# Attention in rounds of eight score tiles, and changed orders of issue in the first stage, in a four-layer float32 kernel

## The chip, the cores and the metric

The kernel runs on one core of one Trainium2 chip. Its time is the device time of one execution in microseconds (us): the median of three runs is 2684.59, from 2683.01 to 2685.78. A profile is taken of one further execution.

The engines' names are those of the profile: PE is TensorE (matmul), PEld its weight loads, DVE is VectorE, ACT is ScalarE, POOL is GpSimd, SP is the engine that issues the DMAs. SBUF is the on-chip working memory, PSUM the memory into which TensorE writes.

## What is computed

The reference passes x (4 images of 512 channels, 64 x 64 positions, float32) through four layers. Only the first matters here:

```python
t = jnp.einsum('oc,bchw->bohw', w_qkv, x)          # key, query, value: 64 channels each
scores = jnp.einsum('bdk,bdq->bkq', key_, query)   # 4096 x 4096 for each image
attn = jax.nn.softmax(scores, axis=1)
out = jnp.einsum('bdk,bkq->bdq', value, attn)
out = jnp.einsum('oc,bchw->bohw', w_out, out)
return scale * out + x
```

Layer 1 is a bottleneck of convolutions whose weights are mixed from eight experts by a router; layer 2 is a linear attention with softplus features; layer 3 is a gate by the sigmoid of a discounted cumulative sum along rows and columns, added to its input.

## The kernel before

The four images (batches) are worked on one after the other. TensorE's order is written out by hand for the whole program (`manual_schedule` of PE around everything, L1074). ACT's and DVE's orders are written out in some stretches only. Where an engine's order is not written out, a planner orders its instructions before the launch, by their place in the program and by its own estimate of when each is ready. In every case an engine carries out its instructions strictly in the order that was fixed, and a semaphore wait of one holds all behind it. Memory is handed out by the planner too: a tile of a pool with n buffers waits for an earlier tile's last reader.

**First stage, `Projections`.** An image is four pairs of blocks (`xs[0]` to `xs[3]`, 128 x 4 x 1024). The keys and queries of two pairs are made together from seven products (numbers 1 to 7) instead of eight, so some inputs are differences that DVE makes first. `steps` (L229) is the written order: a digit is a product on TensorE (L304); `t4`, `n5` and so on are two subtractions on DVE (L252), `t` for this couple of pairs, `n` for the next; `v` is a value product (L260), `cp` its two copies by ACT (L266), `tr` its turning by TensorE and two copies by DVE; `seed`, `e2`, `e3` are copies of the accumulator `y` by ACT; `c11` is four copies by ACT from the first half of the PSUM tile `zy` into the keys (L290); `c22` is one DVE addition of the other half of `zy` and e3 into the queries (L326); `c12` and `c21` are DVE's two remaining results. Product 3 writes the half of `zy` that c22 reads. Two key copies of the second couple are left for later (`key_copies`), those of the first are the step `k`. DVE's and ACT's orders are written out here.

**Attention, `layer0`.** There are 128 tiles: 4 query pairs of 32 key tiles. `scores(i)` makes a tile of 128 keys by 1024 queries: two score matmuls into a PSUM pair (pool tag "s", three buffers), an exponential on ACT (L368) into slot i % 12 of the ring, and the running sum on DVE (L373). `values(i)` multiplies the ring's slot by the values into a bank that collects a query pair (two buffers). The profile shows each matmul as two records, so a tile of scores is four records and a tile of values four. The tiles go in groups of six: the scores of group g, then the values of group g-1. When a pair's values are complete, `sums` follows (two `den` matmuls with ones, L396, a reciprocal on DVE, L399, and three small DVE operations), and for the first two pairs four `out_step`s: an out product (L424) into a PSUM pair, and its addition to x on DVE (L429). They are kept in the list `late`, and up to two are issued in each group, between the scores and the values. The first group is followed by the left key copies and, in batch 0, by the router's transposes (L172). `pool` (L442) is one ACT pass over a piece of x in each of eight groups. The sum product of the last pair, `inverse_sums`, stands before the values of tile 124. In this loop only PE's and ACT's orders are written out; DVE's is the planner's.

**Last stage, `layer3`.** Eight blocks go through products, scans and gates; `last_steps` (L1015) is the written order for the last block of an image, of which only the gate is left. Among DVE's steps there are `g first` (needs sigmoid 0 on ACT), `g second` (three operations and an output) and `g third` (needs sigmoid 1; three operations and an output). The first products of the next image stand among them.

**The ACT table.** The exponentials need a function table that the sigmoid's place doesn't hold; its load is issued at the start of `layer0` (L342). In batch 0 the load follows a square root.

Of the kernel before, what the change touches and what calls it, by code (L numbers as in the profile page):

```python
# [22 lines left out]
NT = HW // P  # L23
TPB = NB // P
NPAIR = NBLK // 2
# [9 lines left out]
BQ2, BK2 = 48, 49  # L35
NPRM = 50
RING = 12

R2 = 2 * ROWS

# [5 lines left out]
def unshifted(ctx: ExitStack, tc: tile.TileContext, fits, x, wqkv_t, wout_t, router_t,  # L46
# [3 lines left out]
    nc = tc.nc  # L50
# [9 lines left out]
    def pair_psum(name):  # L60
        return ps.tile([P, 2, NB], F32, tag="s", name=name, bufs=3)

    def bank(name, shape=(P, NB)):
        return ps.tile(list(shape), F32, tag="acc", name=name)

    def four(name):
        return fourp.tile([P, 2, NB], F32, tag="four", name=name)

    def block(name, shape=(P, NB)):
        return blkp.tile(list(shape), F32, tag="blk", name=name)  # L70
# [31 lines left out]
    def col(i, n=1):  # L102
        return prm_sb[:, i:i + n]
# [46 lines left out]
    groups = [(0, 1, G1, B1, M1, V1), (1, 1, G2, B2, M2, V2), (2, KC, G3, B3, M3, V3)]  # L150
# [15 lines left out]
    def router_of_values():  # L166


        wo_t = pair_psum("wo_t")
        wot_sb = block("wot_sb")  # L170
        for kc in range(KC):
            nc.tensor.transpose(wo_t[:, 0, kc * P:(kc + 1) * P], wout_sb[:, kc * P:(kc + 1) * P], ident)  # L172
        nc.vector.tensor_copy(wot_sb, wo_t[:, 0, :])

        def products():
            wr = pair_psum("wr_p")[:, 0, 0:E]
            for kc in range(KC):
                nc.tensor.matmul(wr, wot_sb[:, kc * P:(kc + 1) * P], router_sb[:, kc, :],
                                 start=kc == 0, stop=kc == KC - 1)
            nc.vector.tensor_scalar(wr_sb, wr, col(SCALE), 1.0 / HW, ALU.mult, ALU.mult)  # L180
        return products

    def load_experts(b, j, n, pool, tag, pack=True):
        if pool is xpool:
            ex = places[NPAIR][:, 0:n, :].rearrange("p n (q g c) -> p n q g c", q=4, g=2)
            nc.sync.dma_start(ex, packed[:, j:j + n])
        elif pack:
            ex = pool.tile([P, n, 4, 2, P], F32, tag=tag, name=f"ex_{b}_{j}")
            nc.sync.dma_start(ex, packed[:, j:j + n])
        else:  # L190
            ex = pool.tile([P, n, E, P], F32, tag=tag, name=f"ex_{b}_{j}")
            nc.sync.dma_start(ex, experts[j:j + n].rearrange("n p e c -> p n e c"))
        return b, j, n, ex
# [18 lines left out]
    class Projections:  # L212
# [14 lines left out]
            nc.vector.tensor_tensor(self.w[3], a12, self.w[6], ALU.subtract)  # L227

        def steps(self, b):  # L229
            first = "v1 cp01 5 1 seed v2 t6 t4 n5 6 n6 e2 2 7 e3 c11 c22 tr01 n7 4 c21 3 c12 n4"  # L230
            if b == 0:
                first = "zero v0 1 seed t5 v1 cp01 t6 5 2 t7 t4 6 e2 v2 7 e3 c11 c22 tr01 n5 n6 n7 4 c21 3 c12 n4"
            return first.split(), "5 1 seed k v3a 6 e2 2 v3b cp23 7 e3 c11 c22 tr23 4 c21 3 c12".split()

        def key_copies(self):
            while self.left:
# [102 lines left out]
    def layer0(b, xs, pro):  # L339


        tc.keep_in_program_order(nc.scalar.preload_act_table_set("natural_log_exp_and_others"))  # L342
        ex0 = load_experts(b, 0, KC, wlate, "late")
        key = bigp.tile([P, HW], F32, tag="big", name=f"key_{b}")
        qv = bigp.tile([P, 2, NPAIR * NB], F32, tag="big", name=f"qv_{b}")
# [3 lines left out]
        with tc.manual_schedule(engines={mybir.EngineType.DVE, mybir.EngineType.Activation}):  # L349
            pro.sum_weights()  # L350
            for pair, steps in zip(((0, 1), (2, 3)), pro.steps(b)):
                pro.products(xs, pair, steps, key, qry, vt)
        ringx = places[NPAIR].rearrange("p i (h n) -> p i h n", h=2)
        ring = [pro.sums[:, i] for i in range(4)] + [ringx[:, i] for i in range(4)] + pro.fours

# [4 lines left out]
        def scores(i):  # L360
            pr, kt = divmod(i, NT)
            s = pair_psum(f"s_{b}_{i}")
            for h in range(2):
                r = slice(h * D, (h + 1) * D)
                nc.tensor.matmul(s[:, h, :], key[r, kt * P:(kt + 1) * P],  # L365
                                 qry[r, pr * NB:(pr + 1) * NB], start=True, stop=True)
            p = ring[i % RING]
            nc.scalar.activation(p, s, AF.Exp)  # L368
            if kt == 1:
                accs[pr] = four(f"acc_{b}_{pr}")  # L370
                nc.vector.tensor_tensor(accs[pr], ring[(i - 1) % RING], p, ALU.add)
            elif kt > 1:
                nc.vector.tensor_tensor(accs[pr], accs[pr], p, ALU.add)  # L373

        def values(i):
            pr, kt = divmod(i, NT)
            if kt == 0:
                avs[pr] = bank(f"av_{b}_{pr}")
            for h in range(2):
                nc.tensor.matmul(avs[pr][h * D:(h + 1) * D, :], vt[:, kt, :], ring[i % RING][:, h, :],  # L380
                                 start=kt == 0, stop=kt == NT - 1)
            if kt < NT - 1:
                return None
            if pr < NPAIR - 1:
                av = block(f"avsb_{b}_{pr}")
                nc.scalar.copy(av, avs[pr])
                avs[pr] = av
            return pr
# [3 lines left out]
        def inverse_sums(pr):  # L392
            acc = accs[pr]
            den = bank(f"den_{b}_{pr}")
            for h in range(2):
                nc.tensor.matmul(den[h * D:(h + 1) * D, :], ones[:, 0:D], acc[:, h, :],  # L396
                                 start=True, stop=True)
            recs[pr] = block(f"rec_{b}_{pr}")
            nc.vector.reciprocal(recs[pr], den)  # L399

        def sums(pr, early=True):
            if early:
                inverse_sums(pr)
            av, rec = avs[pr], recs[pr]
            o = block(f"o_{b}_{pr}")
            if pr >= NPAIR - 2:
                i = pr - NPAIR + 2
                nc.vector.scalar_tensor_tensor(o, av, 1.0, rec, ALU.mult, ALU.mult, accum_out=osum[:, i:i + 1])
            else:
                nc.vector.tensor_tensor(o, av, rec, ALU.mult)  # L410
            outs[pr] = o
            if early:
                sum_range(pr)
# [19 lines left out]
        def out_step(pr, m):  # L433
            add_out(pr, m, out_product(pr, m))
# [5 lines left out]
        def pool(pr, kc):  # L440
            xm = xs[pr][:, kc, :]
            nc.scalar.activation(xm, xm, AF.Copy, accum_out=pool_acc[:, kc, pr:pr + 1])  # L442

        groups = [range(i, min(i + RING // 2, NPAIR * NT)) for i in range(0, NPAIR * NT, RING // 2)]
        late = []
        with tc.manual_schedule(engines={mybir.EngineType.Activation}):
            for g, group in enumerate(groups):
                for i in group:
                    scores(i)
                if 1 < g < 2 + 2 * KC:  # L450
                    pool(NPAIR - 2 + (g - 2) // KC, (g - 2) % KC)
                if g == 0:
                    pro.key_copies()
                    if b == 0:
                        router = router_of_values()
                    continue
                for _ in range(2):
                    if late and late[0][0] < g:
                        late.pop(0)[1]()
                for n, i in enumerate(groups[g - 1]):  # L460
                    if g == len(groups) - 1 and n == 4:
                        inverse_sums(NPAIR - 1)
                    pr = values(i)
                    if pr is not None:
                        late.append((g, lambda pr=pr: sums(pr)))
                        if pr < NPAIR - 2:
                            late += [(g + 1, lambda pr=pr, m=m: out_step(pr, m)) for m in range(KC)]
                if b == 0 and g == 1:
                    router()
        assert not [t for t in late if t[0] < len(groups) - 1], late  # L470


        pooled = small.tile([P, KC], F32, tag="pooled", name=f"pooled_{b}")
# [10 lines left out]

        pr = NPAIR - 1
        ex4 = load_experts(b, 4, 3, bigp, "big")
        for i in groups[-1]:
            values(i)
        ex7 = load_experts(b, 7, 3, xpool, "x")
        wcq = bigp.tile([P, NPIECE + 1 + 4 * NPAIR, P], F32, tag="big", name=f"wc_{b}")  # L490
# [376 lines left out]
    def layer3(b, xs, value_product, value_add, left, weights, wcq):  # L867
# [3 lines left out]
        weights, down, _ = weights  # L871
# [105 lines left out]
        class Gates(Block):  # L977
# [18 lines left out]
            def add_x(self, i):  # L996
# [17 lines left out]
                       ("s3", "s second"))  # L1014
        last_steps = (("g5", "l rows 1", "l rows 0"), ("g1", "g seed", "v 0"), ("g6", "g copy_out 2", "l turn 1"), ("g2",),  # L1015
                      ("g7", "g copy_out 3", "l columns 1", "g fourth", "l turn 0", "l columns 0", "l sigmoid 1",
                       "l sigmoid 0", "v 2"), ("g4",), ("g3", "x", "g third", "g first", "g second"))
        pro = None
        ys = [(pr, m) for pr in range(1, NPAIR) for m in range(KC)]
        nxt = []  # L1020
# [53 lines left out]
    with tc.manual_schedule(engines={mybir.EngineType.PE}):  # L1074
        pro = Projections(0)
        for b in range(B):
            convs = layer1(b, xs, *layer0(b, xs, pro))
            xs, pro = layer3(b, xs, *layer2(b, xs, *convs))
# [455 lines left out]
```

## Time and profile before

| what | us |
|---|---|
| median of three runs | 2684.59 |
| the profiled execution | 2685.98 |
| its span, first to last instruction | 2684.2 |
| TensorE busy (matmul) | 2648.0 |
| DVE busy | 2013.3 |
| ACT busy | 1314.3 |
| first score matmul of batch 0 starts | 57.30 |
| last matmul group ends, last DVE operation ends | 2672.28, 2678.99 |

In the views an instruction line has its start, its length, engine, line of the program, operation, output <- inputs, shape and number, and in brackets how long the engine was idle before it and what ended that. A line of waits has the total, the number of times and the longest. The chain of waits is followed back from the last instruction: where an engine was not waiting, it stands for its own time. Matmuls overlap each other by design, so the start-to-start distance tells the pace and the length does not.

### The profile page before, as it was taken

The page shows a single profiled execution, that of the slowest core. Times are in us where ns is not written, and L with a number is a line of the kernel's source. Part 1 is how long each engine was busy: PE and PEld are TensorE (multiplying, and loading weights), DVE is VectorE, ACT ScalarE, POOL GpSimd, SP SyncE. Part 2 cuts the span into 40 slices and gives each one's busy share as a digit, 9 for nine tenths or more (in the row PEclk, how much of TensorE's full clock was granted, in tenths as well). Part 3 has the DMA queues.
Part 4 walks back from the last instruction along what each step waited for, and adds up shares of the span by engine and source line. Part 5 has one row for each costly group of instructions (what it writes and reads, how often), then busy time and mean ns, then how long its engine had stood idle before and what let it go on. Part 6 is the DMA issues. An engine that isn't in the chain of part 4 may idle for free.

```text
span 2684.2 us, 25782 instructions
## 1 busy us (share of the span) xinstructions
PE 2648.0 (99%) x10048; PEld 1112.5 (41%) x10048; DVE 2013.3 (75%) x2270; ACT 1314.3 (49%) x1510; POOL 12.1 (0%) x26
## 2 busy tenths in 40 slices
PE   8999999999999999999999999999999999999998
PEld 2333364344333346434433334543443333554443
DVE  5688766788778876688877778668886787856787
ACT  3654353545565535345456553535555645363545
POOL 1000000000000000000000000000000000000000
PEclk9999999999999999999999999999999999999999
DMA  5000210021200021002220002101121000210011
GB/s 191 1 1 1 102 32 1 16 110 71 87 1 1 1 102 32 1 29 97 79 79 1 0 1 102 32 1 63 63 94 63 0 1 1 102 32 1 32 47 48
DMA packets 34594, 115.16 MB, mean 43 GB/s; under 512 B 2976, under 2 KB 12192, under 8 KB 32928
## 3 DMA queue, kind: packets, MB, share of 16 engines
q1 hardware_dynamic: 34464, 113.43, 11.4%
q8 instruction: 81, 1.33, 0.2%
q14 instruction: 49, 0.40, 0.1%
HBM read 79.86 MB, written 33.55 MB: 42 GB/s over the span
## 4 chain that ended last, share of the span: by engine, by line
PE 90%; DVE 5%; ACT 4%; issue 1%; DMA 0%; SPq 0%; DVEq 0%; ACTq 0%
PE av L380 17%; PE s L365 16%; PE sx L919 14%; PE zy L919 10%; PE z L663 4%; PE c L638 4%; PE c L566 4%; PE c L615 3%; PE wv L837 2%; PE y L424 2%; PE g L739 2%; PE xtr L724 2%; PE vv L260 2%; PE c2e L615 2%; PE kqz L304 1%; PE kq L304 1%
## 5 line engine op out<-in xcount | busy, mean ns | idle before, releaser
L365 PE MATMUL s<-qv,key 64*128 64x512 f32 x2048 | 463.9, 598 | 4.3 <-ACT x L368 3.1
L373 DVE TENSOR_TENSOR acc<-acc,ring 128x1024 f32<-128x1024 f32 x312 | 381.6, 1223 | 97.4 <-ACT ring L368 69.5
L368 ACT ACTIVATE ring<-s 128x1024 f32<-128x1024 f32 x336 | 317.1, 1038 | 211.0 <-PE s L365 211.0
L380 PE MATMUL av<-ring,qv 128*64 128x512 f32 x1344 | 304.5, 595 | 0.0
L365 PEld LDWEIGHTS s<-qv,key 64*128 64x128 f32 x2048 | 189.1, 186 | 276.2 <-issue 173.6
L373 DVE TENSOR_TENSOR acc<-acc,x 128x1024 f32<-128x1024 f32 x168 | 205.5, 1223 | 99.8 <-ACT x L368 86.6
L368 ACT ACTIVATE x<-s 128x1024 f32<-128x1024 f32 x176 | 172.0, 1041 | 181.9 <-PE s L365 181.9
L919 PE MATMUL sx<-t,x 128*128 128x512 f32 x512 | 238.1, 599 | 1.4 <-ACT e L928 0.8
L380 PEld LDWEIGHTS av<-ring,qv 128*64 128x64 f32 x1344 | 93.2, 137 | 198.7 <-issue 198.7
L380 PE MATMUL av<-x,qv 128*64 128x512 f32 x704 | 167.1, 597 | 0.0
L924 ACT COPY zy<-sx 128x512 f32<-128x512 f32 x64 | 36.5, 570 | 265.9 <-PE sx L919 256.3
L969 DVE TENSOR_TENSOR_SCAN t<-x,t 128x512 f32<-128x512 f32 x128 | 149.1, 1209 | 1.5
L919 PEld LDWEIGHTS sx<-t,x 128*128 128x128 f32 x512 | 94.6, 190 | 132.6 <-issue 121.1
L958 ACT COPY t<-s 128x1024 f32<-128x1024 f32 x64 | 127.5, 1992 | 41.9 <-DVE s L952 41.4
L952 DVE TENSOR_TENSOR_SCAN s<-wc,s 128x512 f32<-128x512 f32 x128 | 145.9, 1201 | 0.0
L928 ACT ACTIVATE e<-sx,prm_sb 128x512 f32<-128x512 f32 x128 | 86.9, 686 | 107.0 <-PE sx L919 107.0
L975 ACT ACTIVATE s<-t 128x1024 f32<-128x1024 f32 x64 | 125.6, 1988 | 12.1 <-DVE t L969 12.0
L919 PE MATMUL sx<-t,wq 128*128 128x512 f32 x256 | 117.0, 597 | 2.1 <-ACT e L928 2.1
L919 PE MATMUL zy<-t,wq 128*128 128x512 f32 x256 | 118.2, 602 | 0.0
L919 PE MATMUL sx<-x,wq 128*128 128x512 f32 x256 | 117.1, 595 | 0.0
L919 PE MATMUL zy<-x,x 128*128 128x512 f32 x256 | 116.2, 594 | 0.0
L663 PE MATMUL z<-x,wqk_sb 128*64 128x512 f32 x512 | 115.8, 597 | 0.0
(228 smaller groups left out, 3445.8 us busy)
## 6 DMA issues: line engine op xcount, KB each, us to landing
out_dram<-s SPq DMA_DIRECT2D x64, 512.0 KB, 2.6
x<-in_x_dram SPq DMA_DIRECT2D x14, 2048.0 KB, 8.7
ex<-in_packed_dram SPq DMA_DIRECT2D x4, 2048.0 KB, 7.5
ex<-in_experts_dram SPq DMA_DIRECT2D x4, 2048.0 KB, 7.8
wq<-in_wproj_t_dram SPq DMA_DIRECT2D x32, 256.0 KB, 5.1
ex<-in_packed_dram SPq DMA_DIRECT2D x4, 1536.0 KB, 6.2
ex<-in_experts_dram SPq DMA_DIRECT2D x4, 1536.0 KB, 6.8
x<-in_packed_dram SPq DMA_DIRECT2D x4, 1536.0 KB, 8.2
```

The lines of the kernel that those rows point to most:

```text
L365: nc.tensor.matmul(s[:, h, :], key[r, kt * P:(kt + 1) * P], qry[r, pr * NB:(pr + 1) * NB], start=True, stop=True)
L368: nc.scalar.activation(p, s, AF.Exp)
L373: nc.vector.tensor_tensor(accs[pr], accs[pr], p, ALU.add)
L380: nc.tensor.matmul(avs[pr][h * D:(h + 1) * D, :], vt[:, kt, :], ring[i % RING][:, h, :], start=kt == 0, stop=kt == NT - 1)
L566: nc.tensor.matmul(y[:, h, :], wc[:, kc, :], xs[pr][:, kc, h * NB:(h + 1) * NB], start=kc == 0, stop=kc == KC - 1)
L615: nc.tensor.matmul(y[:, lo - a:hi - a], u, v[:, lo:hi], start=dy == 1, stop=dy == 2)
L663: nc.tensor.matmul(z[h * D:(h + 1) * D, i, :], wqk_sb[:, kc, w * D:(w + 1) * D], xs[pair[i]][:, kc, h * NB:(h + 1) * NB], start=kc == 0, s ...
L919: nc.tensor.matmul(y, w[:, c, self.kind, self.j * P:(self.j + 1) * P], v[:, c, :], start=c == 0 and k in (1, 5), stop=c == 1, skip_group_c ...
L952: nc.vector.tensor_tensor_scan(self.half(i, h), along[:, self.j + 2 * i, :], self.half(i, h), 0.0, ALU.mult, ALU.add)
L958: nc.scalar.copy(self.t[i].rearrange("p (w r) -> p w r", w=W), self.s[i].rearrange("p (r w) -> p w r", w=W))
L969: nc.vector.tensor_tensor_scan(th, down[:, i, :], th, 0.0, ALU.mult, ALU.add)
L975: nc.scalar.activation(self.s[i].rearrange("p (r w) -> p w r", w=W), tw, AF.Sigmoid)
```

## The change

It has these parts.

1. Rounds of eight (`ROUND = 8`): the scores of tiles 8g to 8g+7, then values up to tile 8g+3, so values stand four tiles behind and the ring keeps twelve slots. Sixteen rounds instead of 22 groups.
2. In a round the late steps come after the values, and a pair's sum product may come in the same round as its last values. The left key copies come behind the second round's scores; the router's parts come after the values of rounds 1 and 2.
3. The sum product of the last pair stands before the values of tile 121 instead of 124.
4. c22 is issued before c11 in all three written orders; in batch 0, n5 comes before c22 instead of behind the turned values.
5. The ACT table load comes after the first couple of pairs.
6. In the last block, "first" and "second" come before "third".

```diff
-            first = "v1 cp01 5 1 seed v2 t6 t4 n5 6 n6 e2 2 7 e3 c11 c22 tr01 n7 4 c21 3 c12 n4"
+            first = "v1 cp01 5 1 seed v2 t6 t4 n5 6 n6 e2 2 7 e3 c22 c11 tr01 n7 4 c21 3 c12 n4"
             if b == 0:
-                first = "zero v0 1 seed t5 v1 cp01 t6 5 2 t7 t4 6 e2 v2 7 e3 c11 c22 tr01 n5 n6 n7 4 c21 3 c12 n4"
-            return first.split(), "5 1 seed k v3a 6 e2 2 v3b cp23 7 e3 c11 c22 tr23 4 c21 3 c12".split()
+                first = "zero v0 1 seed t5 v1 cp01 t6 5 2 t7 t4 6 e2 v2 7 e3 n5 c22 c11 tr01 n6 n7 4 c21 3 c12 n4"
+            return first.split(), "5 1 seed k v3a 6 e2 2 v3b cp23 7 e3 c22 c11 tr23 4 c21 3 c12".split()
...
-        tc.keep_in_program_order(nc.scalar.preload_act_table_set("natural_log_exp_and_others"))
...
                 pro.products(xs, pair, steps, key, qry, vt)
+                if pair[0] == 0:
+                    tc.keep_in_program_order(nc.scalar.preload_act_table_set("natural_log_exp_and_others"))
...
-        groups = [range(i, min(i + RING // 2, NPAIR * NT)) for i in range(0, NPAIR * NT, RING // 2)]
-        late = []
+        late, done = [], 0
         with tc.manual_schedule(engines={mybir.EngineType.Activation}):
-            for g, group in enumerate(groups):
-                for i in group:
+            for g in range(NPAIR * NT // ROUND):
+                for i in range(g * ROUND, (g + 1) * ROUND):
                     scores(i)
                 if 1 < g < 2 + 2 * KC:
                     pool(NPAIR - 2 + (g - 2) // KC, (g - 2) % KC)
-                if g == 0:
+                if g == 1:
                     pro.key_copies()
-                    if b == 0:
-                        router = router_of_values()
-                    continue
-                for _ in range(2):
-                    if late and late[0][0] < g:
-                        late.pop(0)[1]()
-                for n, i in enumerate(groups[g - 1]):
-                    if g == len(groups) - 1 and n == 4:
+                while done < (g + 1) * ROUND - (RING - ROUND):
+                    if done == NPAIR * NT - 7:
                         inverse_sums(NPAIR - 1)
-                    pr = values(i)
+                    pr = values(done)
+                    done += 1
                     if pr is not None:
                         late.append((g, lambda pr=pr: sums(pr)))
                         if pr < NPAIR - 2:
                             late += [(g + 1, lambda pr=pr, m=m: out_step(pr, m)) for m in range(KC)]
                 if b == 0 and g == 1:
+                    router = router_of_values()
+                if b == 0 and g == 2:
                     router()
-        assert not [t for t in late if t[0] < len(groups) - 1], late
+                for _ in range(2):
+                    if late and late[0][0] <= g:
+                        late.pop(0)[1]()
...
-        for i in groups[-1]:
+        for i in range(done, NPAIR * NT):
             values(i)
...
-                       "l sigmoid 0", "v 2"), ("g4",), ("g3", "x", "g third", "g first", "g second"))
+                       "l sigmoid 0", "v 2"), ("g4",), ("g3", "x", "g first", "g second", "g third"))
```

More of the change, by code (lines that the diff above doesn't have):

```diff
@@ L37 @@
 RING = 12
+ROUND = 8
 R2 = 2 * ROWS
@@ L468, in layer0 @@
                 if b == 0 and g == 1:
+                    router = router_of_values()
+                if b == 0 and g == 2:
                     router()
-        assert not [t for t in late if t[0] < len(groups) - 1], late
+                for _ in range(2):
+                    if late and late[0][0] <= g:
+                        late.pop(0)[1]()
+        assert not late
         pooled = small.tile([P, KC], F32, tag="pooled", name=f"pooled_{b}")
```

## The prediction

> **What bounds the kernel now.** I read the page first: its busy times, then the chain.
>
> ```profile
> PE 2648.0 (99%) x10048; PEld 1112.5 (41%) x10048; DVE 2013.3 (75%) x2270; ACT 1314.3 (49%) x1510; POOL 12.1 (0%) x26
> ...
> PE 90%; DVE 5%; ACT 4%; issue 1%; DMA 0%; SPq 0%; DVEq 0%; ACTq 0%
> ```
>
> TensorE sets the end. A change can remove matmul time, waits of TensorE, or the ends of the span, and nothing else counts. No matmul is removed here, so I looked for lost time: TensorE's waits, then the chain inside the attention.
>
> ```profile
> PE kqz L304 <- DVE qv L326: 6.1, 8, 0.8
> PE kqz L304 <- DVE ring L252: 3.8, 1, 3.8
> ...
> PE s L365 <- ACT x L368: 3.1, 3, 1.0
> ```
>
> ```profile
> 87.09 5.35 PE s L365 x24
> 92.44 5.30 PE av L380 x24
> ```
>
> The columns of the first are total, times, longest; of the second, start, length, what. A tile is four matmuls, two pairs side by side. The weight loads of a steady stretch (92.85 to 96.71 us, nine pairs) give 0.429 us a pair, 0.859 a tile. Six tiles are 5.15 us; the chain shows 5.30 for values and 5.35 for scores. So the switch from scores to values costs 0.15 us and the switch back 0.20, inside "busy".
>
> **The change, part by part** (all times us; the sum is made against the profiled execution).
>
> *Switches, gain 6.8.* Before, 22 groups of a batch make 21 switches to values and 20 back. After, 16 rounds (the first already has values of tiles 0 to 3) make 16 and 15. Five of each less: 5 x (0.14 + 0.20) = 1.7 a batch, 6.8 for four. The late steps now follow the values instead of the scores. That moves no switch, since the out product has the scores' form (64*128) and the sum product has the values' form (128*64).
>
> *Start of the attention, gain 6.0.* Groups 0 and 1 of before are one burst of twelve tiles with the key copies of ScalarE between their exponentials:
>
> ```profile
> 729.59 1.26 ACT L290 COPY key<-key 64x512 f32<-64x512 f32 x2
> 730.75 1.92 ACT L368 ACTIVATE x<-s 128x1024 f32<-128x1024 f32 x2
> ...
> 731.82 2.94 PE L365 MATMUL s<-qv,key 64*128 64x512 f32 x12 [1.04 <-ACT x L368]
> ```
>
> Nine tiles run without a gap, the tenth waits 1.04 us and its first pair takes 0.10 longer; smaller gaps of 0.04 follow. Matmul by matmul, the burst loses 1.48 us in this batch and 1.56 in batch 0, where the wait is 1.18 behind the router's copy. After, the copies come behind sixteen exponentials, while four and then eight tiles of values run, and the first tile that needs them is 24. The stall goes: 1.56 + 3 x 1.48 = 6.0.
>
> *Eight tiles in one burst, cost 0.* There are three PSUM pairs, so score i waits for exponential i-3. Exponentials start 0.903 apart (the four at 90.02 take 3.78), scores 0.859, so TensorE runs out of lead. The burst above ran nine tiles on the lead it began with, so eight fit. The Trainium skill, "TensorEngine Tiling (Array Packing)", section PSUM Bottleneck, speaks against longer bursts: tiling speeds up TensorE but not the emptying of PSUM, which may become the bottleneck. By the rule alone each tile of a burst would cost 0.044, 0.35 a round; the row shows no cost up to the ninth tile. Ring slots are free in time: values i-12 are issued before the round's scores, and eight sums at 1.33 (three take 3.88) fill 10.6 of a round of 14.1.
>
> *c22 before c11 in batches 1 to 3, gain 5.9.* The step c22 (DVE L326) needs only e3, but waits for the four key copies of c11:
>
> ```profile
> 28.41 0.58 ACT L312 COPY e<-kq 128x512 f32<-128x512 f32 x1 [4.57 <-PE kq L304]
> 28.90 2.35 ACT L290 COPY key<-kqz 64x512 f32<-64x512 f32 x4
> 31.28 0.69 DVE L326 TENSOR_TENSOR qv<-kqz,e 128x512 f32<-128x512 f32 x1 [8.48 <-ACT key L290]
> 32.03 1.94 PE L304 MATMUL kqz<-x,kqw 128*64 128x512 f32 x8 [0.77 <-DVE qv L326]
> 33.09 5.67 DVE L252 TENSOR_TENSOR ring<-x,x 128x1024 f32<-128x1024 f32 x2
> 37.77 3.02 PE L304 MATMUL kqz<-ring,wqkv_sb 128*64 128x512 f32 x8 [3.80 <-DVE ring L252]
> ```
>
> Both read kqz, and the later reader in program order waited, all eight times. With c22 first it starts at e3's end, some 2.3 earlier, and product 3 finds it done. Each time start to start was 1.36 instead of 0.43, and the next pair 0.05 slow: 0.98. Six times make 5.9. I expect c11 to wait for c22 instead, 0.8 later on ScalarE; nothing of ScalarE is due before the seed 4 us later, or the first exponential, which comes 3 us after the copies' end.
>
> *Batch 0's first stage, gain 7.1.* In the block above the sums n5 (33.09) follow c22 and the transposes, lie under GpSimd's scaling of wv_sb (32.83 to 38.27), and one takes 4.53 instead of 1.22. TensorE waits 3.80, and the next sixteen matmuls take 5.26 instead of 3.43, at half clock. After, n5 stands ahead of c22. The transfer it needs is issued at 8.70 and takes 19.8, so it lands at 28.49. n5 runs 28.5 to 30.9, before GpSimd; c22 ends at 31.5; product 3 starts at 31.54 instead of 32.03, product 5 at 33.3 instead of 37.77, at full clock. Now n6 meets GpSimd and ends near 38.7, when product 6 is due (38.45). Next late are n7, c21 and c12 on DVE (c12 ends 43.3), then two key copies and e2 on ScalarE, 43.9: product 7 is due at 43.6 and starts at 43.95 instead of 49.89. That is 5.9; with the second c22 wait (0.98) scores start at about 50.2 instead of 57.30. Bounds: 5.0 if POOL costs DVE the same 3.3 twice over, 7.4 if nothing is late.
>
> *Table load moved behind the first pair, gain 1.3.*
>
> ```profile
> 688.41 1.28 ACT L342 ACT_TABLE_LOAD   x1
> 689.71 1.07 ACT L266 COPY vsb<-vv 128x512 f32<-128x512 f32 x2
> 690.83 1.51 PE L260 MATMUL vv<-x,wqkv_sb 128*64 128x512 f32 x6 [0.23 <-ACT vsb L266]
> ```
>
> Without the load the value copies end 1.28 earlier and v2 doesn't wait (0.40 start to start, 0.04 after): 3 x 0.44. Behind c11 ScalarE is idle for some 4 us, which hides it; without that cover it would cost 1.28. The Trainium skill, "ScalarE: Activation LUTs", section What ACT_TABLE_LOAD costs, gives 1.283 for the load and 1.38 more for a drain; the row has the load and no drain, the copy starting 0.01 behind it. With the drain the idle 4 us would still hide it.
>
> *Sum product of the last pair, cost 5.9.* It moves from four tiles of values before the end to seven. It needs the sum of tile 127. In the last round (from its first score) DVE's first sum starts at 2.23 (89.25 against 87.02), they are 1.33 apart, and the eighth ends at 2.23 + 7 x 1.33 + 1.23 = 12.8. TensorE is there after eight scores and five values: 13 x 0.859 + 0.24 = 11.4. Wait 1.4, restart 0.1; everything behind it on TensorE waits too. Before, the last group had two tiles and DVE was done. 4 x 1.47 = 5.9. What comes earlier by it, the reciprocal (3.36), was only just in time already, so nothing returns. Lower bound 0. Upper 12, if such a wait halves the clock for 3.4 us as the 3.80 wait did; the 1.04 and 1.18 waits did not, and 1.4 is nearer to these.
>
> *Out products ahead of scores, cost 5.4.* In four rounds a batch two out products now follow the values and the scores follow at once. They fill two of three PSUM pairs, and DVE must add them before scores 1 and 2 of the next round. Before, six tiles of values lay between.
>
> ```profile
> 152.22 1.28 DVE L429 SCALAR_TENSOR_TENSOR x<-y,prm_sb,x 128x1024 f32<-128x1024 f32 x1
> 153.43 0.08 DVE L429 DVE_READ_ACCUMULATOR x<-y,prm_sb,x 128x1 f32 x1
> 153.43 1.28 DVE L429 SCALAR_TENSOR_TENSOR x<-y,prm_sb,x 128x1024 f32<-128x1024 f32 x1
> ```
>
> The adds are 1.21 apart and free PSUM 1.29 after their start. From the round's first score: product 0 ends at 15.20, its add runs 15.25 to 16.54; the second add ends at 17.74. Score 1 is due at 16.76, score 2 at 17.62: late by 0.17, with restart 0.27. In the round after a sum product DVE begins behind a reciprocal (3.36) and three small operations, its eight sums end at 15.4, and the same count gives 0.40. (0.27 + 0.40) x 2 x 4 = 5.4. No row shows it. Below, 0; above, 2.9 a round (46) if score 0 too gets a product's PSUM and the adds stand behind all else on DVE. I take the counted value, nearest to the adds' own row.
>
> *Last block, cost 2.2.* "first" needs sigmoid 0; "third" needs sigmoid 1, done earlier:
>
> ```profile
> 2673.22 1.98 ACT L975 ACTIVATE s<-t 128x1024 f32<-128x1024 f32 x1 [0.93 <-DVE t L969]
> 2674.40 1.28 DVE L998 SCALAR_TENSOR_TENSOR s<-s,prm_sb,x 128x1024 f32<-128x1024 f32 x1
> 2675.60 0.74 DVE L980 SCALAR_TENSOR_TENSOR s<-zy,prm_sb,s 128x512 f32<-128x512 f32 x1
> ```
>
> Before, "third" ran from 2673.04 under that sigmoid. After, DVE idles to 2675.25 and then does all three; the last add ends at 2681.2 instead of 2678.99, and the last output and the end move 2.2. SP's queue only swaps two outputs. Between batches the next batch's sums can fill that hole, and its loads come ahead of both outputs: 0.
>
> **Sum.** 6.8 + 6.0 + 5.9 + 7.1 + 1.3 = 27.1 gained, 5.9 + 5.4 + 2.2 = 13.5 lost: 13.6 net. The profiled execution took 2685.98 (span 2684.2), so about 2672.4; the median of the runs is 1.39 lower, 2684.59, so **2671.0**.
>
> **Rivals.**
> - *The swap doesn't do what it is written for*: DVE waits for c11 whatever the order. Lost: 5.9, and 1.5 of batch 0: 2678.4. For it: the trace can't say why c22 waited. Against: it was the later one all eight times.
> - *The new waits don't come* (DVE gets ahead, or the slots fall otherwise): 11.3 better, 2659.7. Against: DVE's spacing is the same in every round.
> - *Slower*: DVE's out adds become the bound of TensorE. DVE's order in the loop is not written by hand; if the add stands behind the round's sums and the reductions, and score 0 takes the product's PSUM, a clean round loses 1.15 and one after a sum product 2.9: 8 x 4.05 = 32.4 instead of 5.4, 2698. It ends slower than before from 27.1 - 8.1 = 19.0 over 16 rounds, 1.19 a round. For it: DVE is 75% busy. Against: the adds were issued at once behind the sums in the trace.
> - *Several small things*: the clock halves at the new wait, and batch 0 gains 5.0: 2680.
>
> **Chances.** Forecast 0.66 (2665 to 2677), swap idle 0.10, no new waits 0.10, DVE bound 0.07, small things 0.07. The range 2660 to 2681 holds the first, second and last kinds and half the third, 0.88. A measurement of this kernel tells 0.2%, 5.4 us, from no change. Faster: 0.66 + 0.05 + 0.10 = 0.81; same: 0.05 + 0.07 + 0.01 = 0.13; slower 0.06.
>
> **What would show it.** Right: no wait of kqz on L326 or L252, scores starting near 50 us, rounds of 14.1, one wait of about 1.4 for the sum product per batch, small waits of scores on L429, 9 us from the last matmul group's end to the last add instead of 6.7. Wrong: waits of scores on ACT in every round, or c22 still behind c11, or more than 1 us a round on L429.

## The result, and the profile after

The changed kernel's median is 2683.26 us (six runs, 2682.69 to 2684.82) against 2684.32 for the kernel before: a ratio of 0.9997, with a 95% interval of 0.9984 to 1.001. That is no change by the bound of 0.2%, and it lies above the range that the prediction gave. The profiled execution took 2683.29, its span 2681.51 (before: 2685.98 and 2684.20).

The page after has these lines of busy times and of shares of the chain:

```profile
PE 2643.2 (99%) x10048; PEld 1114.9 (42%) x10048; DVE 2016.2 (75%) x2270; ACT 1314.7 (49%) x1510; POOL 12.9 (0%) x26
...
PE 83%; DVE 10%; ACT 3%; issue 2%; DMA 1%; DVEq 0%; SPq 0%; ACTq 0%
```

The matmul count is the same, and DVE's share of the chain has doubled: TensorE waits nearly as much as before (the waits listed add up to 22.9, before to 23.9), for other things. The view of TensorE's waits (total, times, longest) names them:

```profile
PE kqz L305 <- ACT key L291: 9.1, 8, 1.7
PE den L398 <- DVE acc L375: 4.9, 4, 1.2
```

The wait of product 3 for c22 (6.1, eight times) is gone, as is the one for n5 (3.8). In the place of the first there is a wait of the same product for c11, again eight times, and 9.1 in all. The second line is the wait for the last sum product that was predicted.

A cut of both traces at the first matmul of each stage shows where the span changed:

| stage | predicted | measured |
|---|---|---|
| start to the first product of batch 0 | 0 | +0.67 |
| first stage, batch 0 (44.68 before) | -7.1 | -5.55 |
| first stages, batches 1 to 3 (35.77 each before) | -7.2 | +0.65, +0.27, +0.34 |
| attention, four batches (240.16 and 3 x 238.30 before) | -1.5 | -1.27 |
| last matmul to the end | +2.2 | +2.21 |
| sum | -13.6 | -2.69 |

So one row is wrong by 8.5, one by 1.55, and the start moved by 0.67. The attention, the largest part of the diff, did what the sum said.

What product 3 waits for is seen in the second couple of batch 1 after (start, length, and in brackets the idle time before and what ended it):

```profile
712.65 0.59 ACT L313 COPY e<-kq 128x512 f32<-128x512 f32 x1 [0.64 <-PE kq L305]
713.26 0.69 DVE L327 TENSOR_TENSOR qv<-kqz,e 128x512 f32<-128x512 f32 x1 [8.77 <-ACT e L313]
713.99 2.35 ACT L291 COPY key<-kqz 64x512 f32<-64x512 f32 x4 [0.76 <-DVE qv L327]
716.39 1.94 PE L305 MATMUL kqz<-x,kqw 128*64 128x512 f32 x8 [0.90 <-ACT key L291]
```

c22 (L327) starts at e3's end, as predicted. The four copies of c11 (L291), which read the first half of kqz, wait for c22, which reads the second half. Product 3, which writes the second half, then starts 0.05 after the last copy from the first half. The order of the two readers was exchanged, and the sum e3, then one, then the other, is the same.

In the first couple of batches 1 to 3 it is worse, because c22 stands behind the sums n5 and n6 on DVE, and those wait for the last transfer of x:

```profile
690.97 2.36 DVE L253 TENSOR_TENSOR ring<-x,x 128x1024 f32<-128x1024 f32 x2 [0.78 <-DMA x<-in_x_dram]
695.52 0.69 DVE L327 TENSOR_TENSOR qv<-kqz,e 128x512 f32<-128x512 f32 x1
696.24 2.35 ACT L291 COPY key<-kqz 64x512 f32<-64x512 f32 x4 [1.59 <-DVE qv L327]
698.64 1.94 PE L305 MATMUL kqz<-x,kqw 128*64 128x512 f32 x8 [1.74 <-ACT key L291]
```

Transfer, four subtractions (4.6), c22, c11 and product 3 are now one chain. Before, c11 ran while n5 and n6 did, and c22 waited for c11 longer than for n6 (1.83 us in batch 1), so a transfer that came up to that much later was hidden.

### The profile page after: what moved, and what is told of

Read it like the earlier page. It is cut to its first block, busy times and chain, and to the rows that moved or that the text cites. A ratio compares the mean times of both kernels' runs of the same rounds, so it can differ in the third digit from the quotient of the medians.

```text
span 2681.5 us, 25807 instructions
## 1 busy us (share of the span) xinstructions
PE 2643.2 (99%) x10048; PEld 1114.9 (42%) x10048; DVE 2016.2 (75%) x2270; ACT 1314.7 (49%) x1510; POOL 12.9 (0%) x26
## 3 DMA queue, kind: packets, MB, share of 16 engines
q1 hardware_dynamic: 34464, 113.43, 11.3%
## 4 chain that ended last, share of the span: by engine, by line
PE 83%; DVE 10%; ACT 3%; issue 2%; DMA 1%; DVEq 0%; SPq 0%; ACTq 0%
PE sx L920 14%; PE av L382 14%; PE s L367 13%; PE zy L920 10%; DVE acc L375 4%; PE z L664 4%; PE c L639 4%; PE c L567 4%; PE c L616 3%; PE wv L838 2%; PE g L740 2%; PE xtr L725 2%; PE y L426 2%; PE c2e L616 2%; PE kqz L305 1%
## 5 line engine op out<-in xcount | busy, mean ns | idle before, releaser
L382 PE MATMUL av<-x,qv 128*64 128x512 f32 x704 | 159.6, 595 | 0.0
```

## The experiments

Theory: the two halves of kqz are guarded as one tile, so its readers wait for each other, and product 3 for the last of them, whichever half it read. Rival: something else makes product 3 late (DVE's sums, the transfer, a part of the change that stands beside the swap). Medians and 95% intervals of the ratio to the kernel before; where a stage is named, its length is from the two traces.

### The swap alone

```diff
- ... 7 e3 c11 c22 tr01 ...
+ ... 7 e3 c22 c11 tr01 ...
```
(in the three written orders of before)

> The kernel before with c22 ahead of c11 in the three written orders, and nothing else. Theory (product 3 waits for the last reader of either half of kqz, so the swap only exchanges who is last): the eight waits of TensorE for DVE's qv (6.1 in all) become eight waits for ACT's key, 0.9 to 1.7 each, 7 to 9 in all; the time is the same or up to 3 us longer than before. Rival (the swap frees product 3, and in the changed kernel another part, n5 moved or the load moved, made it late): no wait of product 3, 7.8 us faster than before (8 x 0.98).

Measured: 2688.21, ratio 1.0012 (1.0003 to 1.0021), 4.0 longer than before where up to 3 was expected. The waits are of the theory's kind, 11.3 in all instead of 7 to 9:

```profile
PE kqz L304 <- ACT key L290: 11.3, 8, 2.8
```

So the rival that blames another part is out. Two things were not expected. The first stages of batches 1 to 3 are 3.02, 3.56 and 1.39 longer, more than the waits; the run with the old last block, below, shows why. And batch 0's first stage is 5.55 shorter, as much as in the whole change, though n5 wasn't moved. DVE's and POOL's lines of this run:

```profile
30.54 2.35 DVE L252 TENSOR_TENSOR ring<-x,x 128x1024 f32<-128x1024 f32 x2
32.80 5.79 DVE L252 TENSOR_TENSOR ring<-x,ring 128x1024 f32<-128x1024 f32 x2
```

```profile
31.75 7.50 POOL L119 TENSOR_SCALAR wv_sb<-wv_sb,prm_sb 128x2048 f32<-128x2048 f32 x1 [30.27 <-DMA wv_sb<-in_wv_t_dram]
```

With c22 2.5 us earlier, n5 behind it (30.54) keeps its usual 2.35 though GpSimd starts under it, and n6 (32.80) takes the collision.

### n5 alone

```diff
- ... 7 e3 c11 c22 tr01 n5 n6 n7 4 ...
+ ... 7 e3 n5 c11 c22 tr01 n6 n7 4 ...
```
(batch 0 of before)

> The kernel before with n5 ahead of c11 and c22 in batch 0, and nothing else. The swap alone had brought batch 0's first score from 57.3 to 51.6, as early as the whole change. Theory (either edit brings n5 ahead of GpSimd's scaling; they are two ways to the same gain): first score at 51.5 to 52.5, 5 us faster than before, the eight waits of product 3 for qv stay. Rival (the gain needs c22 early): first score at 56 to 57, the time of before.

Measured: 2680.84, ratio 0.9985 (0.9976 to 0.9994). Batch 0's first stage is 5.92 shorter, scores start at 51.93, and the eight waits for qv stay (6.1). The time is 4.4 below that of before in the same comparison (2685.27). The theory holds: swap and n5 are two ways to one gain in batch 0.

### The halves in tiles of their own

```diff
+                    z0 = bank(f"kqf_{self.b}_{pair[0]}")
...
-                    to = y if k in (1, 6, 7, 4) else zy[:, 0 if k == 2 else 1, :]
+                    to = y if k in (1, 6, 7, 4) else z0 if k == 2 else zy[:, 1, :]
...
-                    to_key(lambda h, n0: zy[h * D:(h + 1) * D, 0, :], pair[0])
+                    to_key(lambda h, n0: z0[h * D:(h + 1) * D, :], pair[0])
```
(on before, c11 still ahead of c22; the zero product and the seed go to `z0` as well)

> The kernel before, its order unchanged, with the first half of kqz in a PSUM tile of its own. Theory (the halves are waited for as one tile): c22 no longer waits for c11 and product 3 for neither; the eight waits of 0.8 go, 8 x 0.98 = 7.8 us faster, about 2676.5, less what another PSUM tile costs by making a later tile wait. Rival (c22 is late because e3 or DVE is late, not for c11): product 3 still waits 0.8 eight times, the time is that of before.

Measured: 2679.71, ratio 0.9983 (0.9974 to 0.9992), 4.5 less. The second couple of batch 1, in the order of before:

```profile
715.25 0.59 ACT L313 COPY e<-kq 128x512 f32<-128x512 f32 x1 [0.64 <-PE kq L305]
715.73 2.35 ACT L290 COPY key<-kqf 64x512 f32<-64x512 f32 x4
715.87 0.69 DVE L327 TENSOR_TENSOR qv<-kqz,e 128x512 f32<-128x512 f32 x1 [8.17 <-ACT e L313]
...
717.92 1.46 PE L305 MATMUL kqz<-x,kqw 128*64 128x512 f32 x6
```

c22 runs beside the copies, and product 3 starts without a wait while the last copy is still under way (it ends at 718.08). That is the theory, shown directly: the guard belongs to the tile, not to what is read. First stages of batches 1 to 3 are 1.98, 1.44 and 1.41 shorter; in the last two the transfer came 11.1 after its issue and product 3 waited 0.3 for c22. The full 7.8 was not reached because the tile also cost something: in batch 0 the seed of the second couple now waits for c21, which stands behind GpSimd's collision, and TensorE waits 4.8 for the seed, the next matmuls at half clock.

The Trainium skill, "PSUM — Partial Sum Buffer", section PSUM bank collisions raise a hardware error, gives the rule to guard PSUM by bank and 32-partition quadrant. A bank is 2 KiB a partition there, so 512 float32: each half of kqz is a bank of its own, and the rule asks for no wait between them. The run agrees with that; the wait of before is stricter than the rule.

### c11 early

```diff
- first:  ... 6 n6 e2 2 7 e3 c11 c22 tr01 ...
+ first:  ... 6 n6 e2 2 c11 7 e3 c22 tr01 ...
- second: ... 6 e2 2 v3b cp23 7 e3 c11 c22 tr23 ...
+ second: ... 6 e2 2 c11 v3b cp23 7 e3 c22 tr23 ...
```
(in batch 0 behind e2; once on before, once on the changed kernel)

> The kernel before with c11 directly behind product 2 (in batch 0 behind e2), so ahead of e3 on ACT. Theory: c11 has been done when e3 ends, c22 starts at e3's end, product 3 finds both halves read: 7.8 us faster, about 2676.5; at most 0.2 a couple is given back where the value copies and e3 stand behind c11's 2.35 us. Rival (product 3 is late for another reason): the time of before, and the same eight waits.

Measured: 2676.27, ratio 0.9970 (0.996 to 0.9981), 8.0 less. That this meets the expected 7.8 is partly luck. First stages of batches 1 to 3 are 1.50, 1.40 and 1.50 shorter where 1.96 each was expected, and batch 0's is 5.33 shorter: with c22 early, n5 runs at full speed there as in the swap alone. No wait of kqz is left; in each first couple of these batches 0.4 is given back, where e3 now stands behind c11 and the next product into the accumulator waits for e3.

> The changed kernel with c11 directly behind product 2. Theory: the eight waits of product 3 for ACT's key (9.1 in all, some 9.6 with slow restarts) go; about 2673.7, and the first stage of batches 1 to 3 is 2 to 2.5 us shorter than before's. Rival (in the first couple of batches 1 to 3 c22 is held by DVE's n5 and n6, which wait for the transfer): there 0.5 to 0.9 of the 1.3 to 1.7 stays, so about 2676.

Measured: 2673.82, ratio 0.9963 (0.995 to 0.9977), 9.4 below the changed kernel (1.1 of it lies in the first loads). First stages of batches 1 to 3 are 33.82 to 33.83, 1.95 below before. Second couple of batch 1:

```profile
705.37 2.35 ACT L291 COPY key<-kqz 64x512 f32<-64x512 f32 x4 [1.19 <-PE kqz L305]
...
709.37 0.69 DVE L327 TENSOR_TENSOR qv<-kqz,e 128x512 f32<-128x512 f32 x1 [7.40 <-ACT e L313]
...
711.42 1.03 PE L305 MATMUL kqz<-x,kqw 128*64 128x512 f32 x4
```

c11 needs only product 2; it starts 4.0 ahead of c22 and ends before e3 is made. The rival expected a rest of the wait in first couples; there is none, with the transfer landing 9.5 to 10.3 after its issue.

### The attention's parts

> The kernel before with the attention loop of the change alone (rounds of eight, late steps behind the values, key copies and router later, last sum product seven tiles before the end); first stage, table load and last block as before. Theory (the attention's terms were sized rightly, 6.8 + 6.0 - 5.9 - 5.4 = 1.5 gained): the attention of each batch is 0.3 to 0.4 shorter, the time 1 to 2 us less, which the times alone can't tell from none. Rival (the attention gained more and the rest of the change took it): over 4 us faster than before.

The loop of the change alone on before. Measured: 2682.79, ratio 0.9993 (0.9984 to 1.0002). The attention is 0.61 shorter in batch 0 and 0.32 in the others, 1.6 in all: the theory's size. A further 2.5 came in batch 0's first stage, whose code is that of before: GpSimd's scaling began at 32.18 instead of 32.83, and n5 held TensorE for 3.0 instead of 3.8:

```profile
37.12 2.12 PE L305 MATMUL kqz<-ring,wqkv_sb 128*64 128x512 f32 x8 [3.00 <-DVE ring L253]
```

The wait is 0.8 shorter, and the clock stays at 1.00 behind it, so these eight matmuls take 2.12 and not the 3.02 of before. So that stage of before scatters by some 2 us by itself.

```diff
+                for _ in range(2):
+                    if late and late[0][0] < g:
+                        late.pop(0)[1]()
                 while done < (g + 1) * ROUND - (RING - ROUND):
...
-                for _ in range(2):
-                    if late and late[0][0] <= g:
-                        late.pop(0)[1]()
```
(late steps ahead of the values, on the changed kernel)

> The changed kernel with the late steps of a round ahead of its values, not behind. Theory (an out product that stands directly ahead of scores holds the PSUM pairs until DVE's addition): the stalls of scores 1 and 2 in the four rounds with out products go, 0.3 to 0.7 us each with the slow first pairs, 3 to 5.4 us faster than the changed kernel in all. Rival (the slow first pairs come from the switch between forms of matmul, not from the adds): the losses move behind the out products, the time is the same to 1 us. A sum product may now wait for the reciprocal or the values' bank; that would be seen as a wait of den or av.

Measured: 2678.52, ratio 0.9981 (0.9972 to 0.999), 4.7 below the changed kernel. Each attention is 1.26 shorter, 5.0 in all; the prediction had 5.4. In the changed kernel's trace the first pair of score 1 or 2 came 0.61 to 0.67 after the pair before it instead of 0.43, in the four rounds of a batch; here it doesn't.

```diff
-                    if done == NPAIR * NT - 7:
+                    if done == NPAIR * NT - 5:
```
(sum product of the last pair, on the changed kernel)

> The changed kernel with the sum product of the last pair ahead of tile 123 instead of 121, two tiles (1.72 us) later. Theory: the wait of den for DVE's acc (4.9 in all, 1.2 each) goes, with its restart 1.3 to 1.4 each, 5 to 5.6 us faster; the reciprocal (3.36) is then due in the time of five tiles of values (4.3) and just done. Rival (DVE's chain behind the sum product is what is late): the wait turns up at the end of the attention, the time is the same.

Measured: 2677.46, ratio 0.9975 (0.9965 to 0.9984), 5.8 below. Each attention is 1.45 shorter; the prediction had 1.47. The sum product starts without a wait:

```profile
286.00 1.03 PE L398 MATMUL den<-acc,ones 128*64 128x512 f32 x4
...
287.07 3.36 DVE L401 RECIPROCAL rec<-den 128x512 f32<-128x512 f32 x1 [1.44 <-PE den L398]
```

### The last block, and what it does to the transfer

```diff
-                       ... ("g3", "x", "g first", "g second", "g third"))
+                       ... ("g3", "x", "g third", "g first", "g second"))
```
(on the changed kernel, then with c11 early as well)

> The changed kernel with the old order of the last block, third ahead of first and second. Theory (DVE idles until sigmoid 0 is done): from the last matmul to the last addition 7.3 us instead of 9.45, 2.2 us faster. Rival (the tail belongs to something else): the same time.

Measured: 2686.16, ratio 1.0008 (0.9998 to 1.0017), 2.9 above the changed kernel. The end is 2.16 shorter, as expected. But the first stages of batches 1 to 3 are 2.19, 2.59 and 2.51 longer, which neither side foresaw. SP's lines ahead of batch 1, in this run and then in the changed kernel:

```profile
680.95 0.39 SPq L95 DMA_DIRECT2D x<-in_x_dram  x1
684.45 0.34 SPq L1000 DMA_DIRECT2D out_dram<-s  x1
```

```profile
681.24 0.39 SPq L95 DMA_DIRECT2D x<-in_x_dram  x1
687.71 0.34 SPq L1000 DMA_DIRECT2D out_dram<-s  x1
```

With third first the output is issued 3.5 us behind the load of x (3.9 in batch 1 of some runs), otherwise 6.5. Over all runs here the load then lands 10.35 after its issue (mean of 27, 9.1 to 11.5) against 9.24 (mean of 12, 8.3 to 10.3). With the swap, product 3 waits for what the transfer delays: in the three batches the load landed 0.48, 0.88 and 1.03 later than in the changed kernel, and the wait grew by 0.49, 0.89 and 1.03, to 2.22, 2.23 and 2.44. The other 1.5 to 1.7 of each loss is a second price. The stretches from 696 us on in this run; the last columns are the granted clock, the DMA share and GB/s:

```profile
696.00:700.00 4.00, 1.78 (x10) 0.48 (x8) 4.00 (x6) 3.51 (x5) 0.00 (x0) 1.00 0.02 6
700.00:704.00 4.00, 4.00 (x12) 1.10 (x10) 2.94 (x4) 0.09 (x1) 0.00 (x0) 0.57 0.00 0
```

After the wait TensorE's clock is 0.57, and the 4 us hold 12 matmul records where the changed kernel's hold 22. That also explains the surplus of the swap alone, which has this order of the last block too: its waits in the first couples were 1.96, 2.82 and 2.01, and the clock fell behind the first two, whose stages lost 3.02 and 3.56, and not behind the third, whose stage lost 1.39.

> The changed kernel with c11 behind product 2 and third ahead of first and second in the last block. Without c11's move the old order of the last block had cost 2.2 to 2.6 us in each of batches 1 to 3 and gained 2.2 at the end. Theory (the output issued 3.5 instead of 6.5 us behind the last transfer of x makes that transfer land about 1 us later, and with c11 late TensorE had to wait for it, and above 2 us of waiting ran at half clock; with c11 early nothing waits for it): first stages of batches 1 to 3 stay at 33.8, the end 2.2 earlier, 2671.6. Rival (the old order costs the first stage by DVE's own order): 2 us each lost again, about 2678.

Measured: 2672.71, ratio 0.9953 (0.9939 to 0.9967), 1.1 below the run with c11 early alone. The end is 2.18 earlier; first stages are 33.82, 34.08 and 34.72. The theory holds where the load landed 9.5 after its issue (33.82) and nearly where it landed 10.8 after (34.08); in the third it landed 11.5 after, and product 3 waited 0.7 for c22. So c11 early covers a late transfer up to about 10.5.

### All four together

c11 early, late steps ahead of the values, the sum product at `NPAIR * NT - 5`, and third first, on the changed kernel.

> The changed kernel with c11 behind product 2, the late steps of a round ahead of its values, the last sum product ahead of tile 123, and third ahead of first and second in the last block. Theory (four separate losses, of the sizes measured one at a time): 9.4 + 5.0 + 5.8 + 2.2 = 22.4 below the changed kernel's 2683.3, about 2661; the second batches' first stages stay at 33.8 though the last transfer of x lands a microsecond later. Rival (the losses cover each other, as reciprocal and out additions share DVE): 3 us or more of it is missing, above 2664.

Measured: 2661.80 (five runs, 2660.92 to 2662.63), ratio 0.9913 (0.9899 to 0.9927): 0.9% below the kernel before, the interval well beyond 0.2%. The median is 21.5 below the changed kernel's, the span (2659.05) 22.5. The losses were separate: the rival needed 3 us or more to be missing. The attentions of batches 1 to 3 are 2.72 shorter than after (1.26 and 1.45 make 2.71), that of batch 0 3.07, first stages of batches 1 to 3 are 33.8, and from the start of the last matmul to the last addition it is 7.30. Its busy times and shares of the chain:

```profile
PE 2635.3 (99%) x10048; PEld 1115.3 (42%) x10048; DVE 2014.4 (76%) x2270; ACT 1313.1 (49%) x1510; POOL 12.7 (0%) x26
...
PE 92%; DVE 4%; ACT 3%; DMA 1%; issue 0%; SPq 0%; ACTq 0%; DVEq 0%
```

## Why the prediction was wrong

**The step that failed** is "c22 before c11 in batches 1 to 3": "With c22 first it starts at e3's end, some 2.3 earlier, and product 3 finds it done." The first half is right (713.26 above). The second is wrong: "I expect c11 to wait for c22 instead, 0.8 later on ScalarE; nothing of ScalarE is due before the seed". Product 3 was due, for it waits for c11, 0.90 us in the rows above. The same rows that showed that c22 waited for a reader of the other half pointed to it: a guard of the whole tile binds the next writer too. Predicted -5.9 for six waits, measured +2.6 once the 1.3 of the table load is taken out of the +1.26 of the table. That is 8.5 of the 10.9 that the span misses.

**The first rival** had the right place and the wrong mechanism. It said that DVE would wait for c11 whatever the order. DVE did not wait; TensorE did. Its price, a wait that stays as it was, was too low, since with c11 last the chain begins at the transfer.

**Batch 0's first stage**: -5.55 for -7.1. The end of n5's stall is right, but its 5.9 was put down to n5's move; the swap alone gives the same. Each of the two waits of product 3 stayed (1.00 and 0.90), and these are the missing part. That later sums would take GpSimd's collision instead and be nearly free holds, though it was n7 (5.79 for two) and not n6 as predicted.

**Switches and start of the attention**: not tried one by one. The sum of the attention's gains and losses, -1.5, was measured as -1.27 in the change and -1.6 alone.

**Sum product and out products**: right, 1.45 for 1.47 a batch, and 1.26 for 1.34. The clock stayed full after the wait of 1.24, as assumed.

**Table load**: right. The idle time of v2 behind the value copies is gone in the changed kernel, and first stages with c11 early are 0.45 to 0.54 shorter with the load moved (33.8) than without (34.3 to 34.4); these two kernels differ in the attention and the last block too.

**Last block**: +2.2 at the end is right (2.15). The 0 between batches is wrong: the order sets when the output is issued, with it x landed later, and with c11 last that was worth 2.2 to 2.6 a batch to the change, 0.5 to 1.0 by the landing and the rest by the clock. So this part cost 2.2 and gained about 7, in one kernel alone where the swap had made the transfer matter.

**Start**: the first product began between 12.07 and 13.29 in the runs shown, whatever the edit; +0.67 is this scatter.

What stays open: how the gain of the switches and that of the burst divide, and why the first round of one attention is some 0.35 longer in several runs (batch 0 of the changed kernel, batch 1 of the two runs under "The last block").

## What to carry to other kernels

When two readers of one buffer wait for each other, exchanging them moves the wait to whoever writes next; look for the reader that can run before both are ready, or give the parts buffers of their own. A new order must be followed to the next writer of every tile that it touches, and to the transfer at the head of the chain that it makes. Judge such edits by the length of the stage they are in: here losses and gains of 5 us cancelled in the total, and parts that looked separate (an output's place and a swap two stages later) met in one transfer.

## What the runs showed of the hardware

- **The clock after a short wait.** The length of a wait alone doesn't tell what follows. Behind waits of TensorE of 1.96, 2.22, 2.23, 2.44, 2.82, 3.80 and 4.78 us the clock fell to half; behind 1.90, 2.01 and the 3.00 of the run with the rounds alone it stayed at 1.00. The Trainium skill, "TensorE: Matmul & The Clock Gate", section HAM oscillation — how this bites in real kernels, gives the rule that idle gaps should stay below about 3.4 us. Here 1.96 was enough once; the measurement decides. The clock's records in the traces, which begin some 11 to 13 us into the span, show what tells them apart. Ahead of the end each fall lasts 3.41 us, and the falls of one trace lie whole multiples of 3.413 us apart (700.10 and 1365.70 in the swap alone: 195 of them). On that grid TensorE was idle for 1.96 us or more in the stretch ahead of each fall, and for 1.79 or less in every stretch that no fall followed, in all thirteen traces. The 3.00 lay across a border, 1.79 and 1.21, and so did the 2.01, 0.56 and 1.45. So in these traces it was the place of a wait of 2 to 3 us on the grid that decided whether it cost 1.5 to 1.7 us more. This was worked out from the traces; no edit tested it.
- **A transfer's landing and an output behind it.** 2 MB of x landed 1.1 us later in the mean when an output of 0.5 MB was issued 3.5 instead of 6.5 us behind it. The two sets overlap, and how the two transfers delay each other isn't shown.
- **DVE under GpSimd's scaling.** In each of the thirteen runs one subtraction of 1.22 us took 3.74 to 4.66 under it, and the pair it belongs to 4.87 to 5.80 instead of 2.35; others under it kept their 1.22. The scaling itself took from 5.44 to 7.53; no run shows it without DVE beside it.
